# A two-layer graph network on one core: the mean aggregation in three float32r passes, GpSimd's work in pieces of 256 columns, and a new order of the step

## The chip, the cores and the metric

The kernel runs on one core of a Trainium2 chip. The metric is device time in microseconds, the median of several runs. The engines are named as the profile names them: PE (TensorE, its matmuls; PEld its weight loads), DVE (VectorE), ACT (ScalarE), POOL (GpSimd) and SP (SyncE, whose queue issues nearly all transfers here).

## The reference

The input is x of shape 128 x 128 x 512 (128 graphs, 128 nodes each, 512 features) and a weighted adjacency matrix of 128 x 128 for each graph. Layer 0 has two hypergraph convolutions, layer 1 a mean aggregation. All is float32.

```python
def hypergraph_conv(x, adj, W, b):
    H = (adj != 0)
    w = adj.reshape(N, -1)[:, :C]          # first row of adj
    xw = einsum('ncd,hd->nch', x, W)
    Dn = 1 / einsum('nce,ne->nc', H, w)    # 0 where that is 0
    Be = 1 / H.sum(axis=1)
    m = Be * einsum('nce,nch->neh', H, xw)
    return Dn * einsum('nce,neh->nch', H, m) + b

h = relu(layernorm(x))
y = relu(hypergraph_conv(h, adj, W1, b1))           # 512 -> 1024
y = hypergraph_conv(layernorm(y) * gamma + beta, adj, W2, b2)   # 1024 -> 512
x = x + (y + h)
h = relu(layernorm(x))
deg = adj.sum(-1)
agg = einsum('bij,bjf->bif', adj, h) / max(deg, 1e-6)
x = x + relu(concat([h, agg]) @ W.T)                # 1024 -> 512
```

## The kernel before

One graph is one tile: its 128 nodes lie on the partitions. The weights stay in SBUF. The large products (conv 1, conv 2 and both halves of layer 1's product) are done in three float32r passes: each factor is split into a high part h, a low part l that is scaled up, and a third part d. `product` multiplies h by h and l by l into one PSUM bank, named with an m at the end (rm, gm, bm, am), and d by d into a second (rd, gd, bd, ad). ACT copies the first bank out with a factor, DVE adds the second. Four small products stay in plain float32: ps_s (`node_matrix`, the matrix H B H^T with the weights of D as a 129th column), pz (`conv1_nodes`, that matrix times h), py (`conv2_nodes`) and the aggregation of layer 1 (`aggregate`, ant times gb_t, added into ad).

The split of a left factor is `conv1_high`, `conv1_low`, `conv1_rest` for conv 1 (tile z), and `split_high` with its two inner functions for the other two: `inner_*` for conv 2 (tiles nt, nh, nl, nd, 1024 columns) and `layer1_*` for layer 1 (ht, hh, hl, hd, 512 columns). High parts are made on ACT, low ones on POOL (conv 1's on DVE), third ones on DVE. In conv 1 the third part is made from the first two, both in SBUF.

A left factor must be transposed. The tile is written to DRAM (`trip_out`) and read back in blocks by four transfers (`trip_in`), and DVE turns the 32 x 32 blocks (`turned`: nb to nt, hb to ht). The mean operator takes the same way: `mean_operator` divides adj by its row sums, then an_scratch, anb and ant.

The graphs are software-pipelined. `step(s)` issues one stage each of up to eight graphs, from `load_adjb(s + 4)` to `finish(s - 3)`. The order is written out by hand: nothing is rescheduled, so each engine, and SP's queue, runs its instructions in the order of the calls, waiting on semaphores. `head()` is the same for the first graphs, interleaved with the preparation of the weights (`up`, `high`, `low`, `rest` of the class `Half`); then the steps 3 to 130 follow. PSUM has six rotating banks for the large products and two for the small ones. The pool `left` holds the split left factors, with shared tags; gb_t and h share the tag "B", the block tile hb and a junk tile the tag "hbt".

POOL's work is whole-tile additions and subtractions: `conv1_out` adds the bias b1 to each half of r, `residual` adds h and b2 to x_t, `conv2_bias` adds c0 to g, and the low parts nl and hl. In a step POOL's order is hl, g + c0, r + b1, the two of x_t, r + b1, nl.

Of the kernel before, what the change touches and what calls it, by code (L numbers as in the profile page):

```python
# [23 lines left out]
def gnn_kernel(  # L24
# [33 lines left out]
    P = 128  # L58
# [13 lines left out]

    def bank(name):

        return psum.tile([P, 512], FP, tag="w", name=name)

    def small_bank(name):

        return psum.tile([P, 512], FP, tag="n", name=name, bufs=2)

# [107 lines left out]

    def load_x(g):
        X[g] = pool.tile([P, D], FP, tag="x", name="x_t", bufs=6)  # L190
        nc.sync.dma_start(out=X[g], in_=x[g])

    def load_adj(g):
        ADJ[g] = pool.tile([P, P], FP, tag="adj", name="adj_t", bufs=2)
        nc.sync.dma_start(out=ADJ[g], in_=adj[g])

    def load_adjb(g, queue=nc.sync):
        ADJB[g] = pool.tile([P, P], FP, tag="adjb", name="adjb", bufs=2)
        load_blocks(ADJB[g], adj[g], queue)


    NM, SD, RS = {}, {}, {}

    def centre(key, sums, width):
        NM[key] = nm = pool.tile([P, 1], FP, tag=f"nm{key[0]}", name="nm", bufs=2)
        copy(nm, sums, AF.Copy, scale=-1.0 / width)

    def spread(key, src, junk, width):
        ss = pool.tile([P, 1], FP, tag=f"ss{key[0]}", name="ss", bufs=2)
        copy(junk, src, AF.Square, bias=NM[key], accum_out=ss)  # L210
        SD[key] = sd = pool.tile([P, 1], FP, tag=f"sd{key[0]}", name="sd", bufs=2)
        copy(sd, ss, AF.Sqrt, bias=eps, scale=1.0 / width)  # L212

    def sums(key, src, junk, width, func=AF.Identity):
        sm = pool.tile([P, 1], FP, tag=f"sm{key[0]}", name="sm", bufs=2)
        copy(junk, src, func, accum_out=sm)  # L216
        centre(key, sm, width)

    def scales(g, kind):
        key = kind, g  # L220
        RS[key] = rs = pool.tile([P, 2], FP, tag=f"rs{kind}", name="rs", bufs=2)
        nc.vector.reciprocal(rs[:, 0:1], SD.pop(key))  # L222
        nc.vector.tensor_tensor(rs[:, 1:2], NM.pop(key), rs[:, 0:1], MUL)  # L223

    def normalise(key, dst, src, func):
        rs = RS.pop(key)
        copy(dst, src, func, bias=rs[:, 1:2], scale=rs[:, 0:1])  # L227


    SB, HT, S, DN, H0, Z, PZ = ({} for _ in range(7))  # L230

    def mean_operator(g):
# [4 lines left out]
        nc.vector.tensor_scalar(deg, deg, EPS_DEG, None, MAX)  # L237
# [3 lines left out]

    def mean_out(g):
        ANT[g] = trip_out(ADJ.pop(g), "an")

    def mean_in(g):
# [3 lines left out]

    def mean_transpose(g):  # L250
        anb = ANT[g]
        ANT[g] = pool.tile([P, P], FP, tag="ant", name="ant", bufs=2)
        nc.vector.transpose(ANT[g], anb)

    def incidence(g):
# [13 lines left out]

    def node_matrix(g):  # L270
        ps = small_bank("ps_s")
        nc.tensor.matmul(ps[:, : P + 1], HT.pop(g), SB.pop(g), start=True, stop=True)  # L272
        S[g] = pool.tile([P, P], FP, tag="s", name="s", bufs=4)
        copy(S[g], ps[:, :P], AF.Copy)
        inv = pool.tile([P, 1], FP, tag="inv", name="inv", bufs=2)
        w = ps[:, P : P + 1]
# [5 lines left out]

    def x_sums(g, tag="B"):
        H0[g] = pool.tile([P, D], FP, tag=tag, name="h0")
        sums((1, g), X[g], H0[g], D)
        spread((1, g), X[g], H0[g], D)

    def x_norm(g):
        normalise((1, g), H0[g], X[g], AF.Relu)

    def residual(g, eng=nc.gpsimd):
        eng.tensor_tensor(X[g], X[g], H0[g], ADD)  # L292
        eng.tensor_tensor(X[g], X[g], b2_bc, ADD)  # L293

    def conv1_nodes(g):
# [4 lines left out]

    def conv1_high(g, early=False):
# [14 lines left out]
        def rest():  # L316
            nc.vector.scalar_tensor_tensor(d, h, 2.0**-12, l, MUL, SUB)  # L317

        PZ[g] = low, rest

    def conv1_low(g):
        PZ[g][0]()

    def conv1_rest(g):
# [3 lines left out]
    def product(left, halves, main, name, between=None):  # L328
# [11 lines left out]
        if between:  # L340
            between()
# [7 lines left out]

    def conv1_weights(g, half):  # L350
        PR[g, half] = product(Z[g], w1[half : half + 1], lambda pm: PY.update({(g, half): pm}), "r")

    def conv1_main(g, half):
# [4 lines left out]
    def conv1_out(g, half, eng=nc.gpsimd):  # L358
        cols = HALVES[half]
        r, dn = R[g][:, cols], DN[g]  # L360
        nc.vector.scalar_tensor_tensor(r, PR.pop((g, half)), dn[:, 0:1], r, MUL, ADD)  # L361
        eng.tensor_tensor(r, r, b1_bc[:, cols], ADD)  # L362

    def inner_sums(g):
        sums((2, g), R[g], R[g], DH, AF.Relu)
        spread((2, g), R[g], pool.tile([P, DH], mybir.dt.bfloat16, tag="hbt", name="junk"), DH)

    def inner_norm(g):
# [22 lines left out]

    def inner_out(g):
        NT[g] = trip_out(R.pop(g), "n")

    def inner_in(g):
# [3 lines left out]
    SPLIT = {}  # L399

    def split_high(key, a, tags):
# [8 lines left out]
        def low(eng=nc.gpsimd):  # L410
            SPLIT[key] = part(*l)
            eng.tensor_tensor(SPLIT[key], a, h, SUB)  # L412

        def rest():
# [3 lines left out]
            return [lambda k, v=v: v[:, k, :] for v in (h, low, t)]  # L418

        return low, rest  # L420

    def inner_turn(g):
        NT[g] = turned(NT[g], "t1", "n")

    def inner_high(g):
        NT[g] = split_high(("n", g), NT[g], ("t3", "t2", "t1"))

    def inner_low(g, *eng):
        NT[g][0](*eng)

    def inner_rest(g):
# [3 lines left out]
    def conv2_weights(g, between):  # L435
        PG[g] = product(N_LEFT.pop(g), w2, lambda pm: PY.update({g: pm}), "g", between)

    def conv2_main(g):
        G[g] = t = pool.tile([P, D], FP, tag="A", name="g")
        copy(t, PY.pop(g), AF.Copy, scale=ONE_UP)  # L440

    def conv2_weights_out(g):
        nc.vector.tensor_tensor(G[g], PG.pop(g), G[g], ADD)

    def conv2_bias(g, eng=nc.gpsimd):
        eng.tensor_tensor(G[g], G[g], c0, ADD)  # L446

    def conv2_nodes(g):
        PY[g] = py = small_bank("py")
        nc.tensor.matmul(py, S.pop(g), G.pop(g), start=True, stop=True)  # L450

    def conv2_out(g):
        nc.vector.scalar_tensor_tensor(X[g], PY.pop(g), DN.pop(g)[:, 0:1], X[g], MUL, ADD)  # L453


    def layer1_sums(g):
        H3[g] = pool.tile([P, D], FP, tag="A", name="h3")
        sums((3, g), X[g], H3[g], D)
        spread((3, g), X[g], H3[g], D)

    def layer1_norm(g):
        normalise((3, g), H3[g], X[g], AF.Relu)

    def layer1_trip_out(g):
        H3T[g] = trip_out(H3.pop(g), "h")

    def layer1_trip_in(g):
        H3T[g] = trip_in(H3T[g], "hbt", "h")

    def layer1_turn(g):  # L470
        H3T[g] = turned(H3T[g], "h1", "h")

    def layer1_high(g):
        H3T[g] = split_high(("h", g), H3T[g], ("h2", "h3", "h1"))

    def layer1_low(g, *eng):
        H3T[g][0](*eng)

    def layer1_rest(g):
        H_LEFT[g] = H3T.pop(g)[1]()  # L480

    def layer1_mean(g):
# [335 lines left out]
```

## Time and profile before

| | us |
|---|---|
| median of 3 runs | 2546.36 (2545.41 to 2548.19) |
| the profiled execution | 2543.02 |
| its span, first to last instruction | 2541.1 |
| PE busy | 2490.4 (98%) |
| DVE busy | 2057.7 (81%) |
| ACT busy | 1866.5 (73%) |
| POOL busy | 1324.0 (52%) |

The granted clock of PE was 0.993 over the span. The chain that ended last is PE for 94% of the span. In the middle of the run a step takes 19.23 us (from one gd<-w21d group at 1203.98 us to the next at 1223.22 us).

How to read it: the lengths of matmuls overlap, because a matmul is in the array while the next one starts, so the time that one takes is read from the distance of starts. A group line gives the source line, the engine, the operation, the tiles written and read, the shape and the count; then the busy time in us and the mean length of one in ns; then the idle time of the engine just before, and what ended it. A timeline line gives the start in us from the span's start, the length in us, and the instruction. A float32 matmul stands as two records.

### The profile page before, as it was taken

The page shows a single profiled execution, that of the slowest core. Times are in us where ns is not written, and L with a number is a line of the kernel's source. Part 1 is how long each engine was busy: PE and PEld are TensorE (multiplying, and loading weights), DVE is VectorE, ACT ScalarE, POOL GpSimd, SP SyncE. Part 2 cuts the span into 40 slices and gives each one's busy share as a digit, 9 for nine tenths or more (in the row PEclk, how much of TensorE's full clock was granted, in tenths as well). Part 3 has the DMA queues.
Part 4 walks back from the last instruction along what each step waited for, and adds up shares of the span by engine and source line. Part 5 has one row for each costly group of instructions (what it writes and reads, how often), then busy time and mean ns, then how long its engine had stood idle before and what let it go on. Part 6 is the DMA issues. An engine that isn't in the chain of part 4 may idle for free.

```text
span 2541.1 us, 38324 instructions
## 1 busy us (share of the span) xinstructions
PE 2490.4 (98%) x11024; PEld 1982.9 (78%) x11024; DVE 2057.7 (81%) x4523; ACT 1866.5 (73%) x3864; POOL 1324.0 (52%) x898
## 2 busy tenths in 40 slices
PE   6899999999999999999999999999999999999997
PEld 4687787877877877787787777878788788787875
DVE  7888888888888888888888878888887888888874
ACT  7677777777777777777777777777777777777773
POOL 2255555545545555554554555555455455555552
PEclk9899999999999999999999999999999999999998
DMA  6243344344344334434433433443443443344332
GB/s 171 86 130 121 119 128 127 117 129 128 116 127 127 118 120 128 126 118 129 128 114 128 127 118 119 129 126 117 129 128 113 125 131 119 120 129 125 117 124 74
DMA packets 409651, 311.70 MB, mean 123 GB/s; under 512 B 176736, under 2 KB 340576, under 8 KB 409440
## 3 DMA queue, kind: packets, MB, share of 16 engines
q1 hardware_dynamic: 408608, 309.18, 39.1%
q8 instruction: 87, 1.43, 0.2%
q14 instruction: 124, 1.02, 0.1%
q10 hardware_dynamic: 576, 0.07, 0.0%
q0 software_dynamic: 256, 0.01, 0.0%
HBM read 166.47 MB, written 142.61 MB: 122 GB/s over the span
## 4 chain that ended last, share of the span: by engine, by line
PE 94%; DMA 2%; DVE 1%; ACT 1%; issue 1%; POOL 1%; SPq 0%; DVEq 0%; POOLq 0%; ACTq 0%
PE gm L337 18%; PE rm L337 18%; PE bm L337 9%; PE am L337 9%; PE rd L343 9%; PE gd L343 9%; PE bd L343 4%; PE py L450 4%; PE ad L343 4%; PE pz L298 4%; PE ad L499 4%; PE ps_s L272 1%; DMA x_t<-in_x_dram 0%; DMA hb<-h_scratch 0%; DMA w11r<-in_w1t_dram 0%
## 5 line engine op out<-in xcount | busy, mean ns | idle before, releaser
L412 POOL TENSOR_TENSOR hl<-ht,hh 128x512 fp32r<-128x512 f32 x127 | 164.2, 1293 | 1019.8 <-ACT hh L408 524.6
L216 ACT ACTIVATE h<-x_t 128x512 f32<-128x512 f32 x256 | 161.5, 631 | 334.3 <-DVE x_t L453 318.0
L362 POOL TENSOR_TENSOR r<-r,b_bc 128x512 f32<-128x512 f32 x250 | 376.9, 1508 | 33.2 <-DVE r L361 33.2
L412 POOL TENSOR_TENSOR nl<-nt,nh 128x1024 fp32r<-128x1024 f32 x126 | 303.4, 2408 | 98.1 <-ACT nh L408 98.1
L356 ACT ACTIVATE r<-rm,dinv 128x512 f32<-128x512 f32 x256 | 174.8, 684 | 229.8 <-PE rm L337 229.8
L317 DVE SCALAR_TENSOR_TENSOR z<-z 128x512 fp32r<-128x512 f32 x128 | 227.4, 1777 | 4.4
L227 ACT ACTIVATE h<-x_t,rs 128x512 f32<-128x512 f32 x256 | 208.2, 813 | 12.0 <-DVE rs L223 7.8
L417 DVE SCALAR_TENSOR_TENSOR hd<-hh,hl 128x512 fp32r<-128x512 f32 x128 | 196.4, 1534 | 4.1 <-POOL hl L412 4.1
L314 DVE TENSOR_TENSOR z<-pz,z 128x512 fp32r<-128x512 f32 x128 | 88.5, 691 | 133.3 <-ACT z L310 133.3
L361 DVE SCALAR_TENSOR_TENSOR r<-rd,dinv,r 128x512 f32<-128x512 f32 x256 | 190.5, 744 | 5.5 <-ACT r L356 1.2
L343 PE MATMUL gd<-w20d,nd 128*128 128x512 f32 x512 | 189.3, 491 | 3.4 <-DVE nd L417 3.4
L210 ACT ACTIVATE h<-x_t,nm 128x512 f32<-128x512 f32 x256 | 185.4, 724 | 8.3
L298 PEld LDWEIGHTS pz<-s,h 128*128 128x128 f32 x1024 | 136.5, 195 | 65.6 <-issue 58.9
L293 POOL TENSOR_TENSOR x_t<-x_t,b_bc 128x512 f32<-128x512 f32 x128 | 168.2, 1314 | 20.4 <-DMA adjb<-in_adj_dram 10.5
L292 POOL TENSOR_TENSOR x_t<-x_t,h 128x512 f32<-128x512 f32 x128 | 164.1, 1282 | 27.8 <-ACT h L227 27.7
L222 DVE RECIPROCAL rs<-sd 128x1 f32<-128x1 f32 x384 | 58.7, 153 | 134.4 <-ACT sd L212 134.2
L227 ACT ACTIVATE r<-r,rs 128x1024 f32<-128x1024 f32 x128 | 158.9, 1241 | 6.3 <-DVE rs L223 1.9
L446 POOL TENSOR_TENSOR g<-g,c 128x512 f32<-128x512 f32 x126 | 162.6, 1291 | 0.0
L388 DVE STREAM_TRANSPOSE nt<-nb 128x1024 f32<-128x1024 f32 x128 | 157.6, 1232 | 5.8 <-DMA nb<-n_scratch 4.7
L337 PE MATMUL bm<-w30h,hh 128*128 128x512 f32 x512 | 154.1, 424 | 4.4 <-ACT hh L408 4.4
L417 DVE SCALAR_TENSOR_TENSOR nd<-nh,nl 128x1024 fp32r<-128x1024 f32 x128 | 154.7, 1209 | 2.7 <-POOL nl L412 2.7
L343 PEld LDWEIGHTS gd<-w20d,nd 128*128 128x128 f32 x512 | 96.3, 188 | 75.6 <-issue 31.0
(122 smaller groups left out, 6748.5 us busy)
## 6 DMA issues: line engine op xcount, KB each, us to landing
n_scratch<-r SPq DMA_DIRECT2D x128, 512.0 KB, 2.7
nb<-n_scratch SPq DMA_DIRECT2D x512, 128.0 KB, 2.7
x_t<-in_x_dram SPq DMA_DIRECT2D x128, 256.0 KB, 3.0
h_scratch<-h SPq DMA_DIRECT2D x128, 256.0 KB, 2.0
hb<-h_scratch SPq DMA_DIRECT2D x512, 64.0 KB, 2.0
out_dram<-x_t SPq DMA_DIRECT2D x128, 256.0 KB, 2.0
adj_t<-in_adj_dram SPq DMA_DIRECT2D x128, 64.0 KB, 1.8
an_scratch<-adj_t SPq DMA_DIRECT2D x128, 64.0 KB, 1.6
```

The source lines that it names most:

```text
L210: copy(junk, src, AF.Square, bias=NM[key], accum_out=ss)
L227: copy(dst, src, func, bias=rs[:, 1:2], scale=rs[:, 0:1])
L293: eng.tensor_tensor(X[g], X[g], b2_bc, ADD)
L298: nc.tensor.matmul(z[:, k * P : (k + 1) * P], H0[g][:, k * P : (k + 1) * P], S[g], start=True, stop=True)
L317: nc.vector.scalar_tensor_tensor(d, h, 2.0**-12, l, MUL, SUB)
L337: nc.tensor.matmul(pm, left[i](k), right(i, k), start=(i == 0 and k == 0), stop=(i == 1 and k == kk - 1))
L343: nc.tensor.matmul(pd, left[2](k), right(2, k), start=(k == 0), stop=(k == kk - 1), skip_group_check=True)
L356: copy(R[g][:, HALVES[half]], PY.pop((g, half)), AF.Copy, scale=DN[g][:, 1:2])
L361: nc.vector.scalar_tensor_tensor(r, PR.pop((g, half)), dn[:, 0:1], r, MUL, ADD)
L362: eng.tensor_tensor(r, r, b1_bc[:, cols], ADD)
L412: eng.tensor_tensor(SPLIT[key], a, h, SUB)
L417: nc.vector.scalar_tensor_tensor(t, h, 2.0**-12, low, MUL, SUB)
```

## The change

The aggregation of layer 1 gets the three-pass form of the other products. `mean_transpose` splits ant into three parts (ACT makes the high one, `mean_rest` the two others on DVE), with a factor 4096 that `mean_operator` puts in; gb_t is split by `split_high` into bh, bl and bd (ACT, POOL, DVE). Two of the three matmuls go into the bank am, the third into ad. So am and ad are copied out after the aggregation, at the start of the next step, and the result is added up in its own tile o, which is stored from there. All of POOL's large work goes through `combine`, in instructions of 256 columns. The third part of conv 1 is made from PSUM and the high part. `node_matrix` copies all 129 columns to SBUF, and the weights of D are worked out from there in `node_scale`. The calls of a step and of the head stand in a new order; sums and spreads are separate calls, and so is the bias of conv 1. Each stage is done at most once for a graph, so that the steps begin at -4 and skip what the head has done. Buffers: adj and ant have one buffer instead of two, gb_t shares the tag "hbt", o and the junk tile share "junk".

```diff
+    def combine(eng, dst, a, b, op):
+        width = 256 if eng is nc.gpsimd else dst.shape[1]
+        for c in range(0, dst.shape[1], width):
+            s = slice(c, c + width)
+            eng.tensor_tensor(dst[:, s], a[:, s], b[:, s], op)
...
     def mean_operator(g):
-        nc.vector.tensor_scalar(deg, deg, EPS_DEG, None, MAX)
+        nc.vector.tensor_scalar(deg, deg, EPS_DEG, 1.0 / 4096.0, MAX, MUL)
...
     def mean_transpose(g):
-        ANT[g] = pool.tile([P, P], FP, tag="ant", name="ant", bufs=2)
-        nc.vector.transpose(ANT[g], anb)
+        full = pool.tile([P, P], FP, tag="ant", name="ant")
+        nc.vector.transpose(full, anb)
+        parts = pool.tile([P, 3, P], FP, tag="anp", name="anp").bitcast(FR)
+        ANT[g] = h, l, d = [parts[:, i] for i in range(3)]
+        copy(h, full, AF.Copy, scale=DOWN / 4096.0)
+        def rest():
+            nc.vector.scalar_tensor_tensor(l, h, -4096.0, full, MUL, ADD)
+            nc.vector.scalar_tensor_tensor(d, h, -4097.0, full, MUL, ADD)
...
     def node_matrix(g):
-        S[g] = pool.tile([P, P], FP, tag="s", name="s", bufs=4)
-        copy(S[g], ps[:, :P], AF.Copy)
+        s = pool.tile([P, P + 1], FP, tag="s", name="s", bufs=4)
+        copy(s, ps[:, : P + 1], AF.Copy)
+        S[g] = s[:, :P]
+        DN[g] = s[:, P : P + 1]
+    def node_scale(g):
-        w = ps[:, P : P + 1]
+        w = DN[g]
...
         def rest():
-            nc.vector.scalar_tensor_tensor(d, h, 2.0**-12, l, MUL, SUB)
+            nc.vector.scalar_tensor_tensor(d, h, ONE_UP, pz, MUL, SUB)
...
     def residual(g, eng=nc.gpsimd):
-        eng.tensor_tensor(X[g], X[g], H0[g], ADD)
-        eng.tensor_tensor(X[g], X[g], b2_bc, ADD)
+        combine(eng, X[g], X[g], H0[g], ADD)
+        combine(eng, X[g], X[g], b2_bc, ADD)
...
+    def layer1_mean_high(g):
+        GB[g] = split_high(("b", g), GB[g], ("h2", "h3", "h1"))
...
     def aggregate(g):
-        nc.tensor.matmul(OP[g][1], ANT.pop(g), GB.pop(g), start=False, stop=True,
-                         skip_group_check=True)
+        for i, (left, right) in enumerate(zip(ANT.pop(g), GB.pop(g))):
+            nc.tensor.matmul(OP[g] if i == 2 else PY["o", g], left, right, start=False, stop=i > 0,
+                             skip_group_check=True)
+    def layer1_self_out(g):
+        o, pd = OP[g]
+        nc.vector.tensor_tensor(o, pd, o, ADD)
     def finish(g):
-        o, pd = OP.pop(g)
-        nc.vector.tensor_tensor(o, pd, o, ADD)
-        nc.vector.scalar_tensor_tensor(X[g], o, 0.0, X[g], MAX, ADD)
-        nc.sync.dma_start(out=out[g], in_=X.pop(g))
+        o = OP.pop(g)[0]
+        nc.vector.scalar_tensor_tensor(o, o, 0.0, X.pop(g), MAX, ADD)
+        nc.sync.dma_start(out=out[g], in_=o)
```

The new order of a step, several calls to a line:

```python
def step(s):
    layer1_self_main(s - 4); conv2_bias(s - 2); layer1_self_out(s - 4); x_spread(s + 1)
    layer1_turn(s - 3); layer1_high(s - 3); conv1_weights(s, 0); inner_in(s - 1)
    finish(s - 4); layer1_low(s - 3); mean_out(s - 3); conv2_nodes(s - 2)
    scales(s + 1, 1); node_scale(s + 1); conv2_out(s - 2); x_norm(s + 1)
    conv1_main(s, 0); layer1_rest(s - 3); conv1_out(s, 0); layer1_sums(s - 2)
    conv1_weights(s, 1); conv1_nodes(s + 1); inner_turn(s - 1); layer1_mean(s - 3)
    layer1_spread(s - 2); conv1_main(s, 1); conv1_high(s + 1); conv1_out(s, 1)
    inner_high(s - 1); layer1_self(s - 3); load_adj(s - 2); load_x(s + 2); mean_in(s - 3)
    residual(s + 1); conv1_bias(s, 0); load_adjb(s + 3); conv1_bias(s, 1); inner_low(s - 1)
    scales(s - 2, 3); conv1_low(s + 1); layer1_norm(s - 2); layer1_mean_main(s - 3)
    inner_sums(s); conv1_rest(s + 1); layer1_mean_out(s - 3); layer1_mean_high(s - 3)
    inner_spread(s); mean_transpose(s - 3); mean_operator(s - 2); layer1_mean_low(s - 3)
    inner_rest(s - 1); conv2_weights(s - 1); scales(s, 2); incidence(s + 2); x_sums(s + 2)
    mean_rest(s - 3); layer1_trip_out(s - 2); layer1_mean_rest(s - 3); conv2_main(s - 1)
    inner_norm(s); layer1_trip_in(s - 2); inner_out(s); node_matrix(s + 2)
    aggregate(s - 3); conv2_weights_out(s - 1)
```

In the head, the preparation of w3 is spread differently around the first graphs; the core of it:

```diff
         w3[0].high(1)
...
-        w3[1].low(0)
-        w3[1].up(1)
-        w3[1].high(1)
-        w3[1].low(1)
-        residual(3)
-        incidence(4)
-        x_sums(4)
-        scales(4, 1)
-        layer1_turn(0)
+        w3[0].low(0)
+        conv2_out(1)
...
+        w3[1].low(0)
+        w3[1].up(1)
+        w3[1].high(1)
+        mean_in(0)
+        load_adj(1)
+        residual(3)
+        x_sums(4)
+        x_spread(4)
+        scales(4, 1)
+        x_norm(4)
+        incidence(4)
+        layer1_turn(0)
+        w3[1].low(1)
...
-        step(3, done=(conv1_weights, conv2_bias, conv2_nodes, conv2_out,
-                      layer1_low, layer1_rest))
-        for s in range(4, N + 3):
+        for s in range(-4, N + 5):
             step(s)
```

## The prediction

> **What bounds the kernel now.** I read the page first (busy time, the 40 slices, the chain that ended last), then the busy time by stretches, then one step of each engine's timeline, then the groups of instructions.
>
> ```profile
> PE 2490.4 (98%) x11024; PEld 1982.9 (78%) x11024; DVE 2057.7 (81%) x4523; ACT 1866.5 (73%) x3864; POOL 1324.0 (52%) x898
> PE   6899999999999999999999999999999999999997
> PEclk9899999999999999999999999999999999999998
> 800.00:1200.00 400.00, 399.79 (x1789) 319.56 (x1788) 326.94 (x724) 297.72 (x623) 218.86 (x147) 1.00 0.39 124
> ```
>
> The last line is the stretch from 800 to 1200 us: its length, then PE, PEld, DVE, ACT, POOL busy, clock, DMA. PE has no gap there and runs at the full granted clock; DVE is at 327 of 400, ACT at 298, POOL at 219. In the middle only fewer PE cycles can shorten the step. The ends differ: the first slice is 6, the last 7.
>
> ```profile
> 1220.53 1.07 PE L337 MATMUL gm<-w21l,nl 128*128 128x512 f32 x4
> 1221.44 1.02 PE L499 MATMUL ad<-gb_t,ant 128*128 128x512 f32 x2
> 1221.89 1.48 PE L343 MATMUL gd<-w20d,nd 128*128 128x512 f32 x4
> 1223.22 1.07 PE L343 MATMUL gd<-w21d,nd 128*128 128x512 f32 x4
> 1229.84 1.02 PE L450 MATMUL py<-g,s 128*128 128x512 f32 x2
> 1230.69 1.05 PE L298 MATMUL pz<-s,h 128*128 128x128 f32 x8
> ```
>
> This is PE's timeline: start, length, group. Lengths overlap, so I use starts. Four float32r matmuls take 1221.44 - 1220.53 = 0.91, so one is 0.227 us. The float32 aggregation and the four after it take 1223.22 - 1221.44 = 1.78; less 0.91 the aggregation is 0.87. Float32 py is 0.85. A step repeats after 19.23 us (gd<-w21d at 1203.98 and 1223.22).
>
> ```profile
> L412 POOL TENSOR_TENSOR hl<-ht,hh 128x512 fp32r<-128x512 f32 x127 | 164.2, 1293 | 1019.8 <-ACT hh L408 524.6
> L412 POOL TENSOR_TENSOR nl<-nt,nh 128x1024 fp32r<-128x1024 f32 x126 | 303.4, 2408 | 98.1 <-ACT nh L408 98.1
> L317 DVE SCALAR_TENSOR_TENSOR z<-z 128x512 fp32r<-128x512 f32 x128 | 227.4, 1777 | 4.4
> L417 DVE SCALAR_TENSOR_TENSOR hd<-hh,hl 128x512 fp32r<-128x512 f32 x128 | 196.4, 1534 | 4.1 <-POOL hl L412 4.1
> L417 DVE SCALAR_TENSOR_TENSOR nd<-nh,nl 128x1024 fp32r<-128x1024 f32 x128 | 154.7, 1209 | 2.7 <-POOL nl L412 2.7
> L361 DVE SCALAR_TENSOR_TENSOR r<-rd,dinv,r 128x512 f32<-128x512 f32 x256 | 190.5, 744 | 5.5 <-ACT r L356 1.2
> ```
>
> The two POOL rows lie on a line: 1115 ns per 512 columns and 178 ns fixed. On DVE, hd with 512 columns takes longer than nd with 1024. The timelines show why:
>
> ```profile
> 1208.48 1.29 POOL L446 TENSOR_TENSOR g<-g,c 128x512 f32<-128x512 f32 x1
> 1209.72 1.74 POOL L362 TENSOR_TENSOR r<-r,b_bc 128x512 f32<-128x512 f32 x1
> 1208.81 1.51 DVE L417 SCALAR_TENSOR_TENSOR hd<-hh,hl 128x512 fp32r<-128x512 f32 x1
> ```
>
> hd starts inside POOL's g<-g,c, ends 0.55 after it, and stretches the next POOL instruction from 1.29 to 1.74. An instruction of DVE that reads two SBUF tiles and one of POOL take turns.
>
> **The change part by part.**
>
> *Aggregation.* Out: 0.87 us of PE. In: three float32r matmuls, 3 x 0.227 = 0.68. Py loses pz as its follower and takes over the return from float32 to float32r, which ad's 0.87 holds and py's 0.85 does not: 0.02. Net 0.17 per graph, x 128 = 22 us, all on the path, since PE has no gap. The float32 kinds that stay (py, pz, ps_s) are counted alike on both sides. New period: 19.23 - 0.17 = 19.06.
>
> *What the three passes need.* ACT: bh, 128x512 (0.615, row of hh), and the split of ant, 128x128 (0.255, row of s): 0.87, so 14.4 (298 of 400, of 19.23) becomes 15.2. POOL: bl. DVE: bd (0.69 unblocked, row x_t<-o,x_t) and two of 128x128 (0.29 each, row sb<-adjt,cnt): 1.27. All are ready before the aggregation only if the chain below holds.
>
> *z from PSUM.* z<-z, 1.78 with the wait for POOL, becomes an instruction of one PSUM and one SBUF source like r<-rd: 0.74. DVE -1.04. With the 1.27 it stays near 16 of 19.06. Nothing on PE by itself: DVE work is hidden under PE.
>
> *Pieces.* Per step POOL had seven instructions (six of 512, one of 1024); it gets 18 of 256. The trace has no such row. Lower end: half of 1.29, 0.645. Upper end: 0.645 with the whole 178 ns doubled, 0.82. I take the line: 178 + 558 = 0.735, started every 0.69 (1.29 instructions start every 1.25). 18 x 0.735 = 13.2 us instead of 10.2, beside PE; the limit is not the sum but the chain.
>
> *The new order's chain.* From the end of conv2_weights (call it 0): node_matrix and three passes end at 0.92, plus about 0.16 for the result to arrive; ACT o (0.58), DVE o (0.68), DVE ht (0.70), ACT hh (0.615) with handoffs: hl starts on POOL at 3.7. Then 14 pieces to the end of nl (hl 2, residual 4, bias 4, nl 4): 9.7, plus about 0.45 where hd cuts in: 13.85. DVE nd: 15.1 unblocked. Scales and incidence take 2.0 (1220.67 to 1222.63 in the trace), so sb is there at 17.1, wanted at 19.06. Then the two of ant (0.6) and bd (0.69): 18.4, wanted by the third pass at 19.06 + 0.24 + 0.45 = 19.75. Slack 1.3 us.
>
> Here a rule counts against the change. By row nd is 1.21, but POOL was idle under it; now bl runs there. The Trainium skill, "SBUF — State Buffer", section "Who interferes with whom", says that a DVE instruction with two SBUF inputs and a GpSimd one that reads SBUF shut each other out for the whole of the first. By the row the slack is 1.3; by the rule nd waits for up to one piece, 0.55 to 0.6, and the slack is 0.7. node_scale, which now reads its weight from SBUF, becomes such an instruction too, at up to 0.5, ahead of hd and off this chain. hd's 1.51 agrees with the rule; I take 0.7. Divided over the 14 pieces, the cover holds up to 0.05 more per piece.
>
> *Queues.* SP issues as many transfers as before. The new wait is that the load of hb waits for the tile of gb_t, thus for POOL's last bl piece, near 16; behind it on SP stand n_scratch, nb and the output. hb's four issues (1.73) and its landing (2.0) end at 19.7, while ht starts near 2.3 of the next step, 21.4: 1.7 spare. adj_t has one buffer, whose next load is behind an_scratch: 1.6 us, while its user is a step away. Output now leaves a step later from its own tile. On ACT nothing new waits long except h3's sums behind conv2_out, at a slack as now. Cost: nothing, under those covers.
>
> *Head.* PE waits add up to 34 us before 107.5. The longest in the middle of it is 5.8 us, ps_s at 86.05 for sb, with two w31l of 1.22 just ahead on DVE. The new order sets one of them and one w30l behind: 2 x 1.14 earlier. The first full steps then lose z<-z's wait (2.50 at 100.89): up to 1.8. I take -4; bounds +3 (some other handoff is later) and -9.
>
> *Tail.* Twice py waits 3.64, since hl (1.26) is ahead of g<-g,c on POOL. With conv2_bias first and in two pieces the wait is 0.7 + 1.4 = 2.1: -1.5 each. Against that: the last two aggregations have nothing to hide under, exposing about 0.9 each, and the o copy (0.58) is after the last one. By these rows -0.6. The row after such a wait (bm at 2497.50, 2.58 instead of 1.07) is the second place for a rule: the skill's "TensorE: Matmul & The Clock Gate", "What's actually happening", has the array at half clock after about 3.4 us without work. Waits of 2.1 would fall below that, and two slow starts of some 1.7 us (from py's start at 2496.94 to bd's at 2501.34 is 4.40, warm 2.66) would go: -4. In the head py followed a wait of 1.09 in 2.05, so short waits are slow too at times. I take -2.
>
> Sum: -22 - 4 - 2 = -28 us. The profiled execution took 2543.0 (span 2541.1 and 1.9 around it): 2515. It is 3.3 below the median of 2546.4, so against that median 2518.
>
> **Rivals.** (1) *PE stays the bound*, 0.74: 2507 to 2528, above. (2) *The chain takes part of the gain*, 0.10: the period stays between 19.06 and 19.2, because a piece costs 0.785 to 0.795 or nd and bd each lose a whole piece to POOL; then 0.1 x 122 steps go back, about 2530, up to 2542. For it: the slack is 0.7 of 19. Against: in the step now, waits of that kind left DVE and ACT idle in their own order and PE still had no gap. (3) *POOL's pieces become the pace*, 0.13: place, the chain from hl to nl; price, 14 times what a piece exceeds; point, about 0.80: 14 x 0.065 = 0.9 uses up the slack and the gain together. At 0.82, my upper end, the period is 19.06 + (1.2 - 0.7) = 19.55: 0.32 over now, x 122 = 39, less 6 at the ends: 2579. For it: no row of 256, eleven more starts per step. Against: both rows lie on one line whose fixed part is already in 0.735. (4) *Three passes cost what one did*, 0.03: if a change of weights by pass cost 0.06 more than in the groups of four, whose every matmul also has its own weights; then only the ends count, 2540.
>
> **Numbers.** Time 2518. The range has case 1 and most of 2, with the bounds of head and tail: 2506 to 2538. About 0.2% (5 us) is what a measurement of this kernel tells from no change. Faster by more: cases 1, nearly all of 2, half of 4: 0.84. Within: 0.04. Slower: case 3 and a rest: 0.12.
>
> **What would show it.** Right: period 19.06 by the starts of gd<-w21d; PE without gaps in the middle; three aggregation matmuls 0.227 apart; POOL rows at 735 ns; z near 744; hd at 0.7 to 1.3, nd above 1.21; node-matrix of graph 5 some 4 us before 107.5; py's last waits near 2. Wrong: PE waiting in every step for DVE bd, sb or nd, with POOL busy over 85% and pieces above 0.8; or matmuls of am and ad more than 0.25 apart.

## The result and the profile after

| | before | after |
|---|---|---|
| median, us | 2546.31 (2545.41 to 2548.19) | 2519.66 (2517.76 to 2521.22) |
| runs | 4 | 4 |
| ratio | | 0.9894, 95% interval 0.9877 to 0.9911 |
| the profiled execution | 2543.02 | 2520.2 |
| its span | 2541.1 | 2518.3 |
| node_matrix of graph 5 starts at | 107.53 | 104.67 |
| node_matrix of graph 127 starts at | 2455.79 | 2434.17 |
| median distance of two node_matrix in between | 19.233 | 19.066 |

The change made the kernel 26.7 us faster; 28 were forecast. The profiled execution of before lies 3.3 below its median, that of after 0.5 above, so the two traces differ by 22.8 only, and no trace shows where the other 3.9 lie. Traces are compared with traces below. The table splits the 22.8: head -2.9, the 122 steps between the two node-matrix starts -18.8, tail -1.1.

From the page of after, the busy times and two rows of slices:

```profile
PE 2473.8 (98%) x11152; PEld 2005.2 (80%) x11152; DVE 2128.6 (85%) x4907; ACT 1984.6 (79%) x4120; POOL 1746.9 (69%) x2291
...
PE   6899999999999999999999999999999999999997
...
PEclk9999999999999999999999999999999999999999
```

Two stretches of its middle (length, then PE, PEld, DVE, ACT and POOL busy, clock, DMA share, GB/s):

```profile
400.00:800.00 400.00, 400.00 (x1827) 326.63 (x1826) 343.21 (x799) 321.33 (x673) 289.13 (x379) 1.00 0.40 125
800.00:1200.00 400.00, 399.43 (x1818) 325.51 (x1817) 342.20 (x798) 320.37 (x669) 285.15 (x377) 1.00 0.41 125
```

PE is still the bound in the middle. POOL went from 52 to 69% of the span, DVE and ACT are 15 and 23 us busier in the stretch from 800 to 1200, and all of it fits beside PE, but for 0.57 us of idle PE in that stretch. PE's timeline shows the new aggregation:

```profile
1211.27 1.07 PE L394 MATMUL gd<-w21d,nd 128*128 128x512 f32 x4
1212.17 0.38 PE L310 MATMUL ps_s<-sb,adjt 128*128 128x129 f32 x2
1212.31 0.47 PE L604 MATMUL am<-bh,anp 128*128 128x512 f32 x1
1212.62 0.39 PE L604 MATMUL am<-bl,anp 128*128 128x512 f32 x1
1212.85 0.39 PE L604 MATMUL ad<-bd,anp 128*128 128x512 f32 x1
1213.08 1.09 PE L390 MATMUL rm<-w10h,z 128*128 128x512 f32 x4
1214.01 1.07 PE L390 MATMUL rm<-w10l,z 128*128 128x512 f32 x4
...
1230.31 1.07 PE L394 MATMUL gd<-w21d,nd 128*128 128x512 f32 x4
```

From gd<-w21d to gd<-w21d it is 19.04, and there is no gap. The second and third pass take 0.23 each. The first takes 0.31; it follows the float32 ps_s. In before rm<-w10h stood in that place, and its four took 1.01 instead of 0.91.

The groups of instructions whose costs were estimated, now measured, first on POOL, then on DVE. A row gives the mean length in ns after the busy time:

```profile
L78 POOL TENSOR_TENSOR nl<-nt,nh 128x256 fp32r<-128x256 f32 x504 | 357.4, 741 | 4.9 <-ACT nh L471 4.9
...
L78 POOL TENSOR_TENSOR bl<-gb_t,bh 128x256 fp32r<-128x256 f32 x256 | 266.7, 1063 | 10.4 <-ACT anp L279 5.6 <-ACT bh L471 4.8
```

```profile
L480 DVE SCALAR_TENSOR_TENSOR nd<-nh,nl 128x1024 fp32r<-128x1024 f32 x128 | 209.1, 1634 | 19.5 <-POOL nl L78 19.4
...
L480 DVE SCALAR_TENSOR_TENSOR hd<-hh,hl 128x512 fp32r<-128x512 f32 x128 | 114.8, 897 | 2.8 <-POOL hl L78 2.8
...
L368 DVE SCALAR_TENSOR_TENSOR z<-z,pz 128x512 fp32r<-128x512 f32 x128 | 85.9, 671 | 0.0
```

A piece takes 741 ns (735 forecast). Pieces that meet hd or nd are longer (bl has a mean of 1063), and nd went from 1209 to 1634: these are the turns that the prediction charged. z from PSUM takes 671, where 744 was put.

### The profile page after: what moved, and what is told of

The parts are those of the page before. It is cut to its first block, busy times and chain, and to the rows that moved or that the text cites. A ratio compares the mean times of both kernels' runs of the same rounds, so it can differ in the third digit from the quotient of the medians.

```text
span 2518.3 us, 41388 instructions
## 1 busy us (share of the span) xinstructions
PE 2473.8 (98%) x11152; PEld 2005.2 (80%) x11152; DVE 2128.6 (85%) x4907; ACT 1984.6 (79%) x4120; POOL 1746.9 (69%) x2291
## 3 DMA queue, kind: packets, MB, share of 16 engines
q8 instruction: 88, 1.44, 0.2%
## 4 chain that ended last, share of the span: by engine, by line
PE 93%; DVE 2%; DMA 2%; POOL 1%; issue 1%; ACT 1%; SPq 1%; POOLq 0%; DVEq 0%; ACTq 0%
PE rm L390 18%; PE gm L390 18%; PE bm L390 9%; PE gd L394 9%; PE rd L394 9%; PE am L390 9%; PE bd L394 4%; PE ad L394 4%; PE py L522 4%; PE pz L348 4%; PE am L604 2%; PE ad L604 1%; PE ps_s L310 1%; DMA w21r<-in_w2t_dram 0%; POOL bl L78 0%
## 5 line engine op out<-in xcount | busy, mean ns | idle before, releaser
L78 POOL TENSOR_TENSOR g<-g,c 128x256 f32<-128x256 f32 x252 | 181.1, 741 | 518.2 <-DVE g L513 402.3
L78 POOL TENSOR_TENSOR r<-r,b_bc 128x256 f32<-128x256 f32 x500 | 355.8, 741 | 23.1 <-DVE st L240 14.2
L78 POOL TENSOR_TENSOR nl<-nt,nh 128x256 fp32r<-128x256 f32 x504 | 357.4, 741 | 4.9 <-ACT nh L471 4.9
L78 POOL TENSOR_TENSOR hl<-ht,hh 128x256 fp32r<-128x256 f32 x254 | 180.4, 732 | 144.3 <-ACT hh L471 144.3
L78 POOL TENSOR_TENSOR bl<-gb_t,bh 128x256 fp32r<-128x256 f32 x256 | 266.7, 1063 | 10.4 <-ACT anp L279 5.6
L78 POOL TENSOR_TENSOR x_t<-x_t,h 128x256 f32<-128x256 f32 x256 | 240.7, 961 | 46.9 <-ACT h L245 46.8
L245 ACT ACTIVATE h<-x_t,st 128x512 f32<-128x512 f32 x256 | 207.9, 812 | 34.8 <-DVE st L241 19.6
L480 DVE SCALAR_TENSOR_TENSOR nd<-nh,nl 128x1024 fp32r<-128x1024 f32 x128 | 209.1, 1634 | 19.5 <-POOL nl L78 19.4
L229 ACT ACTIVATE h<-x_t 128x512 f32<-128x512 f32 x256 | 160.2, 626 | 59.1 <-DVE x_t L526 57.8
L78 POOL TENSOR_TENSOR x_t<-x_t,b_bc 128x256 f32<-128x256 f32 x256 | 184.6, 741 | 11.7 <-DMA b_bc<-in_b_dram 11.7
L390 PE MATMUL rm<-w11h,z 128*128 128x512 f32 x512 | 189.7, 492 | 0.0
L234 ACT ACTIVATE h<-x_t,st 128x512 f32<-128x512 f32 x256 | 184.9, 722 | 4.3
L245 ACT ACTIVATE r<-r,st 128x1024 f32<-128x1024 f32 x128 | 158.2, 1236 | 0.6 <-DVE st L241 0.5
```

Of the source, the lines that this page charges most:

```text
L78: eng.tensor_tensor(dst[:, s], a[:, s], b[:, s], op)
L229: copy(junk, src, func, accum_out=t[:, 0:1])
L234: copy(junk, src, AF.Square, bias=t[:, 1:2], accum_out=t[:, 2:3])
L245: copy(dst, src, func, bias=t[:, 5:6], scale=t[:, 4:5])
L390: nc.tensor.matmul(pm, left[i](k), right(i, k), start=(i == 0 and k == 0), stop=(i == 1 and k == kk - 1))
L480: nc.vector.scalar_tensor_tensor(t, h, 2.0**-12, low, MUL, SUB)
```

## Experiments

The kernels were timed in three groups (e1 to e4, e5 to e8, f1 to f4), each beside the kernel before, whose median was 2545.24, 2545.69 and 2546.39 there. The ratios are to that median; a difference of two medians of different groups is uncertain by about 1 us. "Period" is the median distance of node-matrix starts between graphs 6 and 124, "excess" what these steps add up to over that median.

| kernel | us | ratio to before, 95% interval | period | excess |
|---|---|---|---|---|
| before | 2546.31 | 1 | 19.233 | 1.6 |
| after | 2519.66 | 0.9894 (0.9877 to 0.9911) | 19.066 | 3.0 |
| e1_fp32_agg | 2533.22 | 0.9952 (0.9940 to 0.9965) | 19.234 | 0 |
| e2_fp32_agg_splits | 2537.13 | 0.9967 (0.9955 to 0.9980) | 19.240 | 0 |
| e8_extra_pass | 2542.16 | 0.9985 (0.9978 to 0.9991) | 19.266 | 1.5 |
| e3_whole | 2533.66 | 0.9955 (0.9941 to 0.9968) | 19.067 | 13.3 |
| e4_128 | 2751.39 | 1.0810 (1.0795 to 1.0825) | 20.963 | 0 |
| e5_z_sbuf | 2525.72 | 0.9920 (0.9907 to 0.9934) | 19.067 | 7.8 |
| e6_before_pieces | 2564.62 | 1.0066 (1.0053 to 1.0079) | 19.353 | 6.4 |
| e7_before_z | 2543.15 | 0.9989 (0.9982 to 0.9995) | 19.233 | 2.0 |
| f1_norm_first | 2518.06 | 0.9890 (0.9875 to 0.9905) | 19.066 | 2.2 |
| f2_whole_norm_first | 2520.30 | 0.9898 (0.9883 to 0.9913) | 19.060 | 0.6 |
| f3_before_pieces_g_first | 2579.83 | 1.0129 (1.0112 to 1.0146) | 19.394 | 18.0 |
| f4_w31l_back | 2520.88 | 0.9902 (0.9887 to 0.9916) | 19.066 | 2.6 |

### The passes: e1, e2, e8

Two kernels put the single float32 aggregation into the changed kernel, e1 without the splits of ant and gb_t, e2 with them made and not used.

```diff
-        for i, (left, right) in enumerate(zip(ANT.pop(g), GB.pop(g))):
-            nc.tensor.matmul(OP[g] if i == 2 else PY["o", g], left, right, start=False, stop=i > 0,
-                             skip_group_check=True)
+        nc.tensor.matmul(OP[g], ANT.pop(g), GF.pop(g), start=False, stop=True,
+                         skip_group_check=True)
```

> The changed kernel with the aggregation alone put back to one float32 matmul: ant and gb_t are not split (ACT copies gb_t in the place of bh, nothing of it is left on POOL and DVE). Theory A, PE's own work is the time: the 0.17 us per graph come back, 22 us, less about 1 at the end where POOL and DVE no longer stand before the last aggregations: 2539 to 2542, period 19.23. Theory B, the gain is that POOL and DVE shut each other out less: both get lighter here, so the time stays at 2520 or falls.

> As the run before, but with all the work of the two splits still done on ACT, POOL and DVE (its parts are not used). Theory A: that work lies under PE, so the time is that of the run before within 3 us, 2540 to 2543. Theory B, the splits cost time of their own on the path: slower than the run before by 5 us or more.

Both have the old period, 19.234 and 19.240, so the step itself is 0.17 shorter by the passes and by nothing else. But the totals are not what that alone gives, and both lie below their ranges (2539 to 2542 and 2540 to 2543). Each kernel is taken against the before beside it: e1 is 12.0 faster, e2 8.1, after 26.7. So the passes (e2 to after) are worth -18.5. The splits (e1 to e2) cost 3.9; in the traces 2.0 of it stands ahead of graph 5 (102.75 against 104.76), 1.3 behind graph 127. All the rest (before to e1: order, pieces, z, buffers together) is worth -12.0.

The third experiment does the third pass twice.

```diff
-        for i, (left, right) in enumerate(zip(ANT.pop(g), GB.pop(g))):
+        parts = list(zip(ANT.pop(g), GB.pop(g)))
+        for i, (left, right) in enumerate(parts + parts[2:]):
```

> The changed kernel with the third aggregation matmul done twice (its result is then added twice). Theory A: PE gets 0.227 us per graph more, x 128 = 29 us: 2547 to 2551, period 19.28. Rival, PE's records are full but it has hidden slack: less than 10 us more.

PE's timeline at that place:

```profile
1223.17 0.62 PE L605 MATMUL ad<-bd,anp 128*128 128x512 f32 x2
1223.62 1.07 PE L390 MATMUL rm<-w10h,z 128*128 128x512 f32 x4
1224.53 1.07 PE L390 MATMUL rm<-w10l,z 128*128 128x512 f32 x4
```

The time rose by 22.5, less than the 29 expected. The two ad passes take 0.45 instead of 0.23, but the rm<-w10h behind them 0.91 instead of 0.93: 0.20 a step and not 0.227, so 24 over 122 steps, less 1.5 of excess. A pass more makes each step longer by nearly a pass, as it must where PE is the bound.

### Pieces of other widths: e3, e4

```diff
-        width = 256 if eng is nc.gpsimd else dst.shape[1]
+        width = dst.shape[1]
```

> The changed kernel with POOL's work in whole tiles again (width of the tile instead of 256). By the chain of the prediction hl to nl takes 8.6 instead of 9.8 us, while nd on DVE may wait up to 1.15 for a whole bl instead of 0.6: the two cancel. Theory A: 2517 to 2523, period 19.05. Rival, the pieces are what makes the step fit: hd back to 1.5 us and nd at 2.3 make bd late by about 1 us, period near 20, 2600 or more.

```diff
-        width = 256 if eng is nc.gpsimd else dst.shape[1]
+        width = 128 if eng is nc.gpsimd else dst.shape[1]
```

> The changed kernel with pieces of 128 columns. By the line through the measured POOL rows (0.741 for 256, 1.293 for 512) a piece of 128 costs 0.46 and 28 of them from hl to nl take 1.8 us more than 14 of 256. The trace of the changed kernel leaves about 1.1 us from the end of nl to where PE would wait for bd. Theory A with the chain as the next bound: period 19.5 to 20.1, 2575 to 2650. If the chain has more slack than that, or a start costs nothing: 2520.

*Whole tiles* cost 14.0, which neither theory had. In the traces 2.0 of it lie in the head (node_matrix of graph 5 starts at 106.69 instead of 104.67). The rest lies in the middle: most steps take 19.067 as in after, but a quarter of them, mostly in pairs, take 19.1 to 20.2. One such, by the timeline of SP's queue, of DVE and of PE:

```profile
317.41 0.34 SPq L435 DMA_DIRECT2D n_scratch<-r  x1
322.57 1.73 SPq L443 DMA_DIRECT2D nb<-n_scratch  x4
...
326.85 1.25 DVE L450 STREAM_TRANSPOSE nt<-nb 128x1024 f32<-128x1024 f32 x1 [2.23 <-DMA nb<-n_scratch]
...
337.35 0.49 PE L310 MATMUL ps_s<-sb,adjt 128*128 128x129 f32 x2 [0.77 <-DVE sb L304]
```

Here the write of r to n_scratch lasts until nb is read, 5.16 us; in the next step the same two lines are 3.17 apart, and the median is 2.77. So nt starts 2.3 us late (326.85 is 9.6 after ps_s at 317.26, the median is 7.3), nh, nl, nd, incidence and sb follow, and PE waits for sb. The chain ahead of sb is longer than the prediction's: it begins at r, goes through DRAM, and a transfer can be late. In 14 steps of this trace the write takes over a microsecond more than its median, in 2 of after's.

*Pieces of 128* cost 232, far outside the range (2575 to 2650). PE has a new wait. From the waits of PE (us in total, times, longest):

```profile
PE gd L394 <- DVE nd L480: 143.9, 122, 3.9
```

That is 1.2 of the 1.90 us that a step grew by; the rest are slower starts of PE just behind the wait. What makes nd late is a single DVE instruction, as the timelines of POOL and DVE show:

```profile
1209.36 3.40 POOL L78 TENSOR_TENSOR nl<-nt,nh 128x128 fp32r<-128x128 f32 x8
1212.70 1.73 POOL L78 TENSOR_TENSOR bl<-gb_t,bh 128x128 fp32r<-128x128 f32 x4
...
1209.80 4.72 DVE L258 TENSOR_SCALAR adj_t<-adj_t,deg 128x128 f32<-128x128 f32 x1
1214.44 1.21 DVE L480 SCALAR_TENSOR_TENSOR nd<-nh,nl 128x1024 fp32r<-128x1024 f32 x1
```

All instances of it (least, median and longest in ns):

```profile
L258 DVE TENSOR_SCALAR adj_t<-adj_t,deg x128: 285/4658/4735, 82.4 to 2727.4; 128x128 f32<-128x128 f32 x128
```

The small scaling of adj_t, 0.29 us when nothing disturbs it, lasts 4.7 (median 4658 ns), through the rest of nl's eight pieces and all four of bl, and is over when POOL stops. nd stands behind it, though nl had been there since 1212.76. In after, with pieces of 256, the same instruction has a mean of 822 ns. So it was not the sum of POOL's pieces (307 of 400 us busy from 800 to 1200) that decided, but this instruction, which got no turn between short pieces of POOL. No run moved it behind nd or took it away, and why it got no turn is not shown.

### The third part of conv 1: e5, e7

```diff
-            nc.vector.scalar_tensor_tensor(d, h, ONE_UP, pz, MUL, SUB)
+            nc.vector.scalar_tensor_tensor(d, h, 2.0**-12, l, MUL, SUB)
```

> The changed kernel with the third part of conv 1 made from two SBUF tiles again. It is 0.67 us now and would be up to 1.3 with a wait for one POOL piece. DVE is idle 0.3 and 1.3 us just behind it. Theory A: hidden, 2518 to 2523. Theory B, DVE's waits for POOL are on the path: 0.6 x 122 = 75 us, 2590.

E5 is after with the old form, e7 is before with the new one (the diff the other way round).

> The kernel before with the third part of conv 1 made from PSUM and nothing else: DVE loses about 1.0 us a step, 130 us of busy time in all. Theory A: 2544 to 2548, the time does not see it. Theory B: a part of the 130 us comes out, 2535 or less.

In after the old form costs 6.1, which neither theory had: period unchanged, head +0.9, excess 7.8 instead of 3.0. In before the new one gains 2.5 against the before beside it, and the two traces (spans 2541.4 and 2541.1) do not show where: period and ends are the same. From the groups of e5, on DVE:

```profile
L480 DVE SCALAR_TENSOR_TENSOR nd<-nh,nl 128x1024 fp32r<-128x1024 f32 x128 | 222.4, 1738 | 47.9 <-POOL nl L78 47.8
L368 DVE SCALAR_TENSOR_TENSOR z<-z 128x512 fp32r<-128x512 f32 x128 | 161.4, 1261 | 4.4
```

z from SBUF has a mean of 1261 ns, from PSUM 671. The longer z is not what nd waits for: DVE waits for POOL's nl, 47.8 us in all instead of 19.4. The four pieces of nl, which meet z, take 3.29 instead of 2.84 in the median step and end 14.32 after ps_s instead of 13.87, and nd ends 0.2 later. That is the cover that a late transfer lacks: where the write of r to DRAM lands 0.95 late (in the steps at 1044, 1656 and 2268 us of its trace), e5 loses 0.3; after loses nothing where it lands as late (steps at 1041, 1652 and 2262).

### Pieces in the old order: e6, f3

e6 is the kernel before with `combine` in 256 columns for POOL's five kinds of work, nothing else.

```diff
+    def combine(eng, dst, a, b, op):
+        width = 256 if eng is nc.gpsimd else dst.shape[1]
+        for c in range(0, dst.shape[1], width):
...
-        eng.tensor_tensor(G[g], G[g], c0, ADD)
+        combine(eng, G[g], G[g], c0, ADD)
```

> The kernel before with POOL's work in pieces of 256 columns and nothing else. Theory A: PE has no gap there, so nothing to gain; g + c0 ends about 0.3 us later and py has 0.84 us to spare, so nothing to lose: 2544 to 2549. Theory B, shorter locks speed the step: 2535 or less. The z row should fall from 1777 ns to below 1300 all the same.

The z row fell to 1082 ns as expected, but the time followed neither theory: the pieces alone made the old kernel 18.9 us slower than the before beside it, with 0.12 more in every step, and the excess rose from 1.6 to 6.4. Step for step PE loses the 0.12 from py to the bm behind it. POOL's and DVE's timelines at that place:

```profile
1236.06 1.44 POOL L77 TENSOR_TENSOR hl<-ht,hh 128x256 fp32r<-128x256 f32 x2 [7.26 <-DMA adjb<-in_adj_dram]
1237.45 1.89 POOL L77 TENSOR_TENSOR g<-g,c 128x256 f32<-128x256 f32 x2
...
1237.63 1.11 DVE L423 SCALAR_TENSOR_TENSOR hd<-hh,hl 128x512 fp32r<-128x512 f32 x1
```

hl takes 1.44 for 1.29, and hd, which had to wait for the end of all of g before (1.51), now gets its turn between the two pieces (1.11). So g takes 1.89 for 1.29: what DVE wins POOL loses. In the median step g now ends 0.08 ahead of py's start, where it was 0.82 in before, so py waits for g. f3 puts g ahead of hl:

```diff
-        do(layer1_low, s - 3)
         do(conv2_bias, s - 2)
+        do(layer1_low, s - 3)
```

> The kernel before with pieces of 256 and one swap: conv2_bias is issued ahead of layer1_low, so that POOL does g + c0 before hl. With pieces alone the kernel before took 2564.6, and py waited for g<-g,c in each step (0.12 a step): hl takes 1.44 instead of 1.29 and DVE's hd gets its turn between the two pieces of g. Theory (it is that one place): period 19.23 again, 2546 to 2551. Rival (the pieces slow POOL or DVE in general, whatever the order): period stays near 19.35, 2560 to 2566.

That made it worse by another 15. py no longer waits (g ends 1.53 ahead of it). But hl now ends 5.66 after the start of ps_s, not 3.78 as in e6; hd and what stands behind it on DVE come later; nt starts at 9.51, not 7.64, nd ends at 17.32, not 15.68, and gd starts 0.69 after the aggregation instead of 0.45. Most of the 15 is excess (18.0 instead of 6.4), in steps in which gm waits for nh (16 waits, 11.7 us). So the theory of the one place is wrong: in the old order py and nd both need POOL at that moment, and with pieces neither of the two orders tried has both in time.

### Is it POOL's pace or the trip? f1, f2

ACT normalises r only after g<-gm, which waits for PE's last gm. f1 swaps the two calls in after, f2 in e3_whole.

```diff
-        conv2_main(s - 1)
         inner_norm(s)
+        conv2_main(s - 1)
```

> The changed kernel with one swap in the step: inner_norm is issued ahead of conv2_main, so ACT normalises r before it waits for the last gm. In the changed kernel's trace r<-r,st starts 18.17 us after ps_s, behind g<-gm, which waits 1.0 to 1.4 us for PE; with the swap r ends some 1.2 us earlier and the trip of r through n_scratch to nb starts as much earlier, as far as hb's issues ahead of it on SP's queue allow. Theory C (the longer steps come from a trip that lands late, by up to 2 us over its median of 7.2; what is late then is nt, nl, nd, sb in turn): nt starts near 6.4 us after ps_s instead of 7.58, the longer steps (3.0 us in all) go, period 19.07, 2515 to 2519. Rival D (the longer steps come from POOL's own pace, hl to nl): nl still starts when its turn on POOL comes, 11.26 after ps_s, the longer steps stay, 2519 to 2521. Rival E (g<-gm now comes late for g<-gd, py waits): 2521 to 2530.

> The same swap in the changed kernel whose POOL instructions are whole tiles (2533.7 us without the swap, longer steps of 13.3 us in all, 14 trips through n_scratch over a us later than their median). Theory C (pieces are worth 14 us only because a late trip through DRAM has less cover without them): most of the longer steps go, 2519 to 2525. Rival D (whole tiles of POOL are too slow themselves, by what they block on DVE): stays near 2533, 2530 to 2536.

r<-r,st starts 16.5 after ps_s instead of 18.2 in both (here, as in the expectations, counted from ps_s's weight load, 0.2 ahead of its matmul). f2 is the one that tells: with whole tiles on POOL, as in e3, the excess falls from 13.3 to 0.6 and the time from 2533.7 to 2520.3. The waits of DVE for the trip (us in total, times, longest), in e3:

```profile
DVE nt L450 <- DMA nb<-n_scratch: 42.4, 42, 2.4
```

and in f2:

```profile
DVE nt L450 <- DMA nb<-n_scratch: 6.6, 6, 1.9
```

42 waits became 6. Two things changed. Only 4 writes of r, not 14, were over a microsecond late. And a late one cost less. The write at 1239.1 in e3 landed 2.07 later than the median; nt was 1.98 late, and the two steps from there were 1.14 longer. The write at 1286.6 in f2 landed 2.06 later; nt was 0.92 late, and the two steps were 0.05 longer. So an earlier start takes the late transfer off the path, and does it without pieces.

Theory C says more: that the pieces themselves are cover. The traces do not bear that out. In after DVE waits for nb more often than in e3, with little excess:

```profile
DVE nt L450 <- DMA nb<-n_scratch: 66.3, 109, 2.2
```

The write at 982.3 in after landed 1.80 late; nt was 1.83 late, and the two steps were 1.26 longer, no less than in e3. And in the median step sb is ready 18.19 after the start of ps_s's matmul in after, 18.04 in e3. After has less excess than e3 because 2 of its writes are that late and not 14. Why the writes of e3 are late so much more often was not found. It is not the chip alone: e1, e2 and e4 were timed beside e3 and have no such write in the middle.

In f1 nt starts at 7.10 instead of 7.58 (6.4 was expected), but the excess falls by 0.8 only; 4 of its writes are over a microsecond late. 2518.06 is the lowest median of all; its runs (2516.61 to 2518.65) overlap those of after, so a gain of 1.6 is below what these runs can tell.

### A step of the head put back: f4

```diff
         x_norm(4)
+        w3[1].low(1)
         incidence(4)
         layer1_turn(0)
-        w3[1].low(1)
         layer1_high(0)
```

> The changed kernel with one call of the head put back: the second w31l of 1.22 us stands ahead of incidence of graph 4 on DVE again, as before the change. By the prediction's step for the head (1.14 us for each large instruction that is set behind sb) ps_s of graph 4 starts 1.1 to 1.2 us later than at 84.88, node-matrix of graph 5 about 1.1 later than at 104.67, and the time is 2520 to 2521.5. Rival (the head has another limit behind it): ps_s of graph 4 moves, that of graph 5 by under 0.4, and the time is unchanged.

Two waits of PE's timeline in the head, in after:

```profile
84.88 0.80 PE L310 MATMUL ps_s<-sb,adjt 128*128 128x129 f32 x2 [4.96 <-DVE sb L304]
...
104.67 0.49 PE L310 MATMUL ps_s<-sb,adjt 128*128 128x129 f32 x2 [0.19 <-DVE sb L304]
```

and in f4:

```profile
86.15 0.80 PE L310 MATMUL ps_s<-sb,adjt 128*128 128x129 f32 x2 [6.38 <-DVE sb L304]
...
104.98 0.49 PE L310 MATMUL ps_s<-sb,adjt 128*128 128x129 f32 x2 [0.20 <-DVE sb L304]
```

ps_s of graph 4 moves by 1.27, as the prediction priced it, and 0.31 of that is left 20 us later. In after PE has a wait in between (bd for w30d, 0.83 at 92.71) that f4 does not have. So the rival was right on graph 5: there is another limit behind. The time does not decide: 2520.88 lies in the range of the first theory, but the runs (2519.23 to 2522.44) overlap those of after.

## Why the prediction was right, and where it was not

*Aggregation: right per step, a fifth too large in the sum.* 0.17 a step was forecast, 0.167 measured. The term of 22 was mis-sized in what surrounds it: e2 to after gives 18.5. In the traces before to after gained 20.4 in the middle (0.167 x 122), less 1.4 because the excess rose from 1.6 to 3.0; and from e2 to after the tail lost 1.3, because the last aggregations wait for their splits (0.91 and 0.57 the longest, below).

*What the passes need: hidden in the step, not at the ends.* The splits were costed at nothing, "ready before the aggregation if the chain holds". In the middle that is so. But e1 to e2 shows 3.9, of it 2.0 in the head and 1.3 in the tail. This is the step that failed: the cover named was PE's work, and at the ends PE waits anyway, so that other work there moves its waits. The prediction priced this in the tail alone (0.9 for each of the last two aggregations). In the tail PE's waits over the last 50 us grew from 7.6 (e1) to 9.2 (e2). In the head they grew in places but not in the sum (29.4 ahead of graph 5 in both); PE's busy time grew, from 73.5 to 75.1. One place where it did, by PE's timeline in e1:

```profile
56.77 1.20 PE L385 MATMUL gd<-w20d,nd 128*128 128x512 f32 x4 [2.56 <-DVE nd L471]
```

and in e2:

```profile
57.20 2.08 PE L395 MATMUL gd<-w20d,nd 128*128 128x512 f32 x4 [3.28 <-DVE nd L485]
```

Behind the longer wait the same four matmuls are slow, at a granted clock of 0.50 (57.2 to 59.1); in e1 it is 1.00 there (56.8 to 57.8). Where the rest of the 1.6 lies was not followed. Which of the splits' instructions lengthen the waits was not tried.

*Order, head and tail: half the size.* Forecast -6, measured -12.0 from before to e1. In the traces it is -10.2: head -4.8, tail -3.7, and 1.6 of longer steps that e1 does not have. In the change itself the head shows -2.9 and the tail -1.1, since the splits' 2.0 and 1.3 are in them, and in the tail also the 1.3 for which the aggregations wait. The errors of this and of the splits offset the first: -18.5 + 3.9 - 12.0 is near -22 - 6, and that is partly luck. Of the mechanism named for the head, a w31l and a w30l set behind sb, the w31l is worth 0.3 (f4); the w30l was not tried. In the traces pz's wait behind it fell from 1.72 to 0.71 and a wait of gm for nh of 1.65 is gone; which moved call did that was not tried.

*Tail.* The waits, in PE's timeline:

```profile
2473.63 1.13 PE L522 MATMUL py<-g,s 128*128 128x512 f32 x2 [1.62 <-POOL g L78]
2474.53 1.20 PE L390 MATMUL bm<-w30h,hh 128*128 128x512 f32 x4
...
2499.16 0.47 PE L604 MATMUL am<-bl,anp 128*128 128x512 f32 x1 [0.91 <-DVE anp L282]
...
2503.89 2.08 PE L390 MATMUL bm<-w30h,hh 128*128 128x512 f32 x4 [3.51 <-ACT hh L471]
...
2512.53 0.50 PE L604 MATMUL am<-bl,anp 128*128 128x512 f32 x1 [0.57 <-POOL bl L78]
```

py waits 1.62 twice (2.1 forecast, 3.64 before), and the group behind it is nearly at full speed: from 2474.53 the four of bm take 1.04, at a granted clock of 1.00. Behind the wait of 3.51 the same four take 1.87, at a granted clock of 0.50 (from 2503.9 to 2505.8). In before, the four behind the first wait of 3.64 take 2.37 at 0.53. That is what the Trainium skill's "TensorE: Matmul & The Clock Gate", section "What's actually happening", says of a window of some 3.4 us without work, and the two slow starts behind py did go.

*The chain, and the lock between DVE and POOL: right.* In the median step of after nl ends 13.87 after the start of ps_s (13.85 forecast, from about there) and nd 15.88 (15.1 unblocked, up to 15.7 by the rule). The slack had been cut to 0.7 by the rule of the Trainium skill's "SBUF — State Buffer", section "Who interferes with whom". In after's timelines nd lasts 1.78 where 1.21 was the row without the rule, bd ends at 1212.43, and its matmul starts at 1212.85: 0.42 is left. The rule as used there, a wait for one POOL instruction, does not hold the case of e4, where DVE was shut out for some eleven. The lines of after, from DVE's timeline:

```profile
1207.16 0.59 DVE L258 TENSOR_SCALAR adj_t<-adj_t,deg 128x128 f32<-128x128 f32 x1
1207.67 1.78 DVE L480 SCALAR_TENSOR_TENSOR nd<-nh,nl 128x1024 fp32r<-128x1024 f32 x1
...
1211.13 0.29 DVE L304 TENSOR_SCALAR sb<-adjt,cnt 128x128 f32<-128x128 f32 x1
...
1211.74 0.69 DVE L480 SCALAR_TENSOR_TENSOR bd<-bh,bl 128x512 fp32r<-128x512 f32 x1
```

*z from PSUM.* It was priced at nothing on PE, because DVE's work is hidden. e5 shows 6.1, by way of POOL: a z that reads two SBUF tiles makes nl later.

*The rivals.* PE stayed the bound. The chain took some 3 us back (rival 2, in a few steps and not in all). Rival 3 had named a real edge but the wrong mechanism: at 128 columns the pieces do cost more than the gain, by what they do to adj_t<-adj_t,deg; at 256 a piece is 741 ns, far from 800. And its chain from hl to nl was too short: it left out the trip of r through DRAM, which decides when nl can start in the late steps.

*Queues: costed at nothing, and nearly so.* What the prediction did not ask of SP's queue is how much a transfer varies. The trip from the issue of n_scratch to nt has a median of 7.22 in after and a longest of 9.28, which is more than the slack.

## What to carry to other kernels

Where one engine is the bound, its own instructions can be priced to a few hundredths of a microsecond per step; what goes wrong is the cover, at the ends where there is none and in the steps where a transfer is late. So ask of each hidden chain what its latest transfer does, not only what its median does, and start the transfer earlier before making the instructions behind it shorter. Cutting POOL's instructions into pieces moved waiting from DVE to POOL (e6), so look at which of the two is needed first, and look in the trace whether the other still gets its turn between the pieces (e4).

## What the hardware showed that was not expected

- DVE's adj_t<-adj_t,deg, 0.29 us alone, took 4.7 us beside back-to-back POOL instructions of 128 columns (465 ns each), in nearly every step. Beside pieces of 256 columns (741 ns) it took 0.63 in the median and 2.4 at most, with whole tiles a mean of 0.41. Other DVE instructions of the kernel with 128 columns, hd among them (688 ns), did not suffer.
- Tiny DVE instructions with two SBUF sources wait too: dinv<-s,inv has a mean of 408 ns in after, 939 with whole tiles and 167 with 128 columns, against 158 when its weight came from PSUM.
- The write of r to DRAM (512 KB) takes 2.76 us in most steps, from its issue to that of nb, and up to 4.6 in after, 5.2 in e3. In e3 five of the longest lie 307 us apart (317.4, 624.9, 932.3, 1239.1, 1546.5), which is 16 steps. The late ones of the other kernels with the short step lie about as far apart: 982.3 and 1288.5 in after, 373.5, 680.0 and 985.9 in e5. Why was not found.
- The first float32r matmul behind the float32 ps_s takes 0.31 instead of 0.227.
